# A decoder block on one core: the prologue re-ordered so that attention scores begin behind the first two chunks' layer norms

## The chip, the core and the metric

The kernel runs on one core of a Trainium2 chip. The core has five instruction streams that run side by side and wait for one another through semaphores: TensorE (PE, matrix products and transposes), VectorE (DVE), ScalarE (ACT), GpSimd (POOL), and SyncE (SP, which issues transfers). ACT issues transfers too, from the same stream as its arithmetic. The metric is the device time of one launch in microseconds (us), as a median over runs. The trace is of one profiled launch.

## The reference

`x` is 2 x 1024 x 256 in float32, so 2048 tokens. Three layers follow one another, each added to `x`:

```
n  = layernorm(x)
q, k, v = n Wq, n Wk, n Wv                      (16 heads of 16)
x += affine_layernorm( (softmax(q k^T / 16) + bias[rel]) v )
n  = layernorm(x);  k2, v2 = ctx Wk2, ctx Wv2   (ctx: 2 x 77 x 256)
x += (softmax(mask(n Wq2 k2^T)) v2) Wu + bu
n  = layernorm(x)
x += affine_layernorm( 0.5 gelu(n Ws + bs) + sum over the best 2 of 8 experts of weight * expert(n) )
```

The bias of the first layer is drawn from a table by relative position. The mask of the second layer says which of the 77 context rows count.

## The kernel before, in words

The 2048 tokens lie in SBUF in `xs` as four chunks of 512 (chunks 0 and 1 are batch 0, chunks 2 and 3 batch 1). A chunk's layer norm has these steps: `bn_stats` and `bn_aggr` on DVE give mean and variance, a power of -0.5 on POOL gives the reciprocal deviation (`norm_scale`, L133), the chunk is scaled into a tile `xn`, and `turned` (L188) turns `xn` on PE in two halves, `kc` 0 and 1, and copies each into `xnT`. There are two forms of the scaling: `scale_tokens` (L310) on DVE with the mean and the deviation, and `offsets` (L166) on DVE followed by `scale` (L177) on ACT.

Self-attention is split into 16 units (batch, group of four heads, half of the queries) of eight steps, so 128 steps. Stream A of a step (`stream_a`, L518) makes four scores `sA` on PE, and DVE takes each one's row maximum into `mx` (L533). Ten steps later (`LAG`) stream B makes the scores again, turned and shifted by the maxima (`sB`, L572), ACT takes the exponentials into tiles `pt` (L580), and `times_v` (L584) multiplies them with the values `vaug`. The queries shifted by the maxima, `qB` (L555), are made once in eight steps.

On PE, DVE, ACT and POOL the order of the program text is the order of execution: these four run under a schedule written by hand (`manual_schedule`, L239). Whatever stands ahead of the step loop is the prologue. The table `between` (L905) names the jobs that stand ahead of the scores of a step, inside the loop. All PSUM tiles come from one ring of eight banks in order of use (`one`, L83), so a bank that has not been emptied holds up the PE stream.

The prologue before: transfers are issued on SP and ACT (L245 to L261), `vaug` is cleared by DVE and POOL, constants are made from the identity matrix (`own`, `extra`, `use`, `hsel`), the weights of queries and keys are rearranged by ACT (L282), chunks 0 and 1 are normed and turned, keys and queries of the first four groups are projected (`project`, L490: `wk` and `wq`, each in column halves `j` 0 and 1). Then come the rest of the loads with the bias table (`rest_of_loads`, L288), the mask (`mask_bias`, L472), and keys and values of the context (`context_turn`, `context_keys`, `context_values`). Only then does step 0 begin. Between steps 0 and 7 stand the values of all chunks (`values`, L329) and the layer norms of chunks 2 and 3. `add_values` (L352) sums the values on POOL for the flat part of the bias.

The tiles `cx`, `cwk`, `cwv`, `wv`, `mk` and the raw weights live in a pool `fst` that is closed in step 9; the pool of `pt`, `avs` and `part` then takes the same memory, so that its first users wait for the last users and the loads of `fst`.

A load takes one of eight semaphores in turn; a load that comes eight places later waits until the earlier one has landed.

Of the kernel before, what the change touches and what calls it, by code (L numbers as in the profile page):

```python
# [11 lines left out]
ALU = mybir.AluOpType  # L12
# [3 lines left out]
B = 2  # L16
S = 1024
D = 256
H = 16
DH = 16  # L20
N = B * S
NT = N // P
QT = S // P
# [12 lines left out]
FLAT = 510  # L36
# [4 lines left out]
def decoder_kernel(  # L41
# [27 lines left out]
    nc = tc.nc  # L69
# [17 lines left out]
    moments, tokens = {}, {}  # L87
# [9 lines left out]
    def load_x(c):  # L97
        nc.sync.dma_start(
            out=xs[:, 4 * c : 4 * c + 4, :],
            in_=xf[512 * c : 512 * c + 512, :].rearrange("(t p) d -> p t d", p=P),  # L100
        )

    def load_rows(src, name, cols, pool=const, eng=nc.scalar):
        t = pool.tile([P, 2, cols], F32, name=name)
        eng.dma_start(out=t, in_=src.rearrange("(kc p) f -> p kc f", p=P))
        return t
# [6 lines left out]
    def load_heads(src, name, pool, eng):  # L113
        t = pool.tile([P, 2, H, DH], F32, name=name)
        for kc in range(2):
            eng.dma_start(  # L116
                out=t[:, kc, :, :], in_=src[:, kc * P : (kc + 1) * P, :].rearrange("h p k -> p h k")
            )
        return t.rearrange("p kc h k -> p kc (h k)")
# [42 lines left out]
    def deviation(c, eps=1e-5):  # L162

        tokens[c] = norm_scale(moments[c][1], 4, eps)
# [81 lines left out]
    for name, src in (("wk", a_wk), ("wq", a_wq)):  # L246
        raws[name] = load_rows(src, f"{name}raw", D, fst)
    load_x(1)
    cx = fst.tile([P, B, D], F32, name="cx")
    for b in range(B):  # L250
        nc.sync.dma_start(out=cx[:T2, b, :], in_=context[b])
    cwk = load_heads(c_wk, "cwk", fst, nc.scalar)
    load_x(2)
    cwv = load_heads(c_wv, "cwv", fst, nc.scalar)
    wv = load_rows(a_wv, "wv", D, fst)
    load_x(3)
    for a in range(8):
        nc.sync.dma_start(out=flat_of[16 * a : 16 * a + 16, :], in_=a_relT[:, FLAT : FLAT + 1])
    mk = fst.tile([P, NT, T2], I32, name="mk")
    nc.sync.dma_start(out=mk, in_=mask.rearrange("b (t p) k -> p (b t) k", p=P))  # L260
    beta_a = load_bcast(a_beta, "beta_a")  # L261

    nc.vector.memset(vaug[:, : QT // 2], 0.0)
    nc.gpsimd.memset(vaug[:, QT // 2 :], 0.0)
    nc.gpsimd.memset(vaug.rearrange("p k h r b -> p (k h) r b")[:, :, DH, :], 1.0)
    i32 = ident.rearrange("p (g r) -> p g r", r=32)
    for i in range(2):
        nc.vector.tensor_reduce(own[i], i32[:, :, DH * i : DH * i + DH], AX.XY, ALU.add)
# [2 lines left out]
    nc.vector.tensor_reduce(  # L271
        hsel, ident.rearrange("p (a j r) -> p j a r", a=2, j=4), AX.XY, ALU.add
    )
    nc.vector.tensor_scalar(hsel, hsel, 0.25, None, ALU.mult)
    for name, raw in raws.items():
        c0 = {"wk": 2048, "wq": 2560}[name]
        w = scrap[:, c0 : c0 + 512].rearrange(
# [10 lines left out]
    def rest_of_loads():  # L288
        nc.vector.tensor_copy(tab[:, FLAT - 7 :], flat_of.to_broadcast([P, M_TAB - FLAT + 7]))
        for a in range(8):  # L290
            nc.sync.dma_start(
                out=tab[16 * a : 16 * a + 16, : FLAT + 1 - a], in_=a_relT[:, a : FLAT + 1]
            )
        for m in shifts:
            nc.gpsimd.memset(m, 0.0)
        nc.gpsimd.memset(vx, 0.0)
# [9 lines left out]
    def measure_tokens(c):  # L306
        mv = stats(xs[:, 4 * c : 4 * c + 4, :], 4)
        tokens[c] = mv, norm_scale(mv, 4, 1e-5)

    def scale_tokens(c):  # L310
        mv, r = tokens[c]
        xn = work.tile([P, 4, D], F32, tag="xn", name="xn")
        for t in range(4):
            nc.vector.tensor_scalar(
                xn[:, t, :],
                xs[:, 4 * c + t, :],
                mv[:, t, 0:1],
                r[:, t : t + 1],
                ALU.subtract,
                ALU.mult,  # L320
            )
        tokens[c] = mv, r, xn

    def turn_tokens(c):

        for kc in range(2):
            turned(c, kc, by_dve if kc == 0 and c < 2 else by_act)

    def values(c, u):  # L329

# [139 lines left out]
            )  # L470

    def mask_bias():  # L472
        nc.vector.tensor_scalar(mb, mk, 0, -1000000000.0, ALU.is_equal, ALU.mult)
        nc.vector.tensor_reduce(live, mb, AX.X, ALU.max)
        nc.vector.tensor_scalar(live, live, 0.0, None, ALU.is_ge)

# [409 lines left out]
    def shared(c, u):  # L886
# [16 lines left out]


    between = {  # L905
        0: [lambda: values(0, 0)],
        1: [lambda: values(0, 1), lambda: measure_tokens(2)],
        2: [lambda: values(1, 0), lambda: scale_tokens(2), lambda: turn_tokens(2)],
        3: [lambda: values(1, 1), lambda: measure_tokens(3)],
        4: [lambda: values(2, 0), lambda: scale_tokens(3), lambda: turn_tokens(3)],  # L910
        5: [lambda: values(2, 1)],
        6: [lambda: values(3, 0)],
        7: [lambda: values(3, 1), add_values],
        16: [flat_bias],
        20: [lambda: bias_half(2, 0)],
        22: [lambda: bias_half(2, 1)],
# [3 lines left out]
        30: [lambda: bias_turn(3, 0), lambda: bias_turn(3, 1)],  # L920
    }
    between.update({40 + 4 * c: [lambda c=c: add_rows(c, beta_a)] for c in range(4)})
    measure_tokens(0)
    scale_tokens(0)
    turn_tokens(0)
    measure_tokens(1)
    scale_tokens(1)
    project(0, "wk", 0)
    project(0, "wq", 0)
    turn_tokens(1)  # L930
    project(0, "wk", 1)
# [643 lines left out]
```

## Time and profile before

| | |
|---|---|
| runs | 1022.87, 1023.93, 1017.91 us; median 1022.87 |
| profiled launch | 1017.8 us, its span 1016.1 us |
| granted PE clock, mean | 0.95 |
| busy: PE, DVE, ACT, POOL | 897.9, 604.8, 529.4, 398.5 us |
| prologue, up to the first values product | 31.79 us |
| first product of stream B (`sB`) | starts at 70.38 us |

The share of busy time says which engine has most work in the mean over the span; it is no answer for the first 70 us, which this change touches. There, read the timeline and the chain of waits: a line of the timeline gives start, duration, engine, line of the kernel, operation, tile written and tiles read, the count of merged instructions, and in brackets the idle time ahead and who ended it. A `q` behind an engine's name (ACTq, SPq) is its sequencer at issuing a transfer.

### The profile page before, as it was taken

What the parts mean: (1) busy time and instruction counts of PE and PEld (TensorE: products, weight loads), DVE (VectorE), ACT (ScalarE), POOL (GpSimd) and SP (SyncE); (2) the same over time, 40 slices, a digit from 0 to 9 for tenths busy, and PEclk for the clock granted to TensorE, in tenths of its full rate; (3) what the DMA queues carried; (4) which work ended last, traced back from release to release, by engine and by line L of the source; (5) the groups of instructions that cost most, each with busy time, mean ns of one, the idle gap of its engine ahead of it and who ended that gap; (6) DMA issues with size and microseconds to landing.
All of it is one profiled execution on the core that took longest, in us unless ns stands there. A gap on an engine that the chain in (4) does not pass through costs nothing.

```text
span 1016.1 us, 15875 instructions
## 1 busy us (share of the span) xinstructions
PE 897.9 (88%) x5948; PEld 520.5 (51%) x5948; DVE 604.8 (60%) x1197; ACT 529.4 (52%) x1051; POOL 398.5 (39%) x321
## 2 busy tenths in 40 slices
PE   3889999999999999999965999997999999998900
PEld 1553334333333333333323667786887888887800
DVE  6787558877888887987689998670110110101157
ACT  1327568867887787786852777413232222233301
POOL 3032223443334354344366897004334422222124
PEclk9989999999999999999985999998999999999955
DMA  8200000000000000000000000127446446699252
GB/s 175 48 1 1 2 1 2 1 2 1 2 1 2 1 1 2 1 1 2 1 1 17 2 22 22 43 78 280 148 175 213 160 168 201 224 321 325 80 170 83
DMA packets 65143, 75.62 MB, mean 74 GB/s; under 512 B 17948, under 2 KB 57017, under 8 KB 65057
## 3 DMA queue, kind: packets, MB, share of 16 engines
q1 hardware_dynamic: 50512, 62.31, 19.0%
q0 software_dynamic: 3360, 8.79, 2.3%
q10 hardware_dynamic: 11184, 3.41, 1.4%
q8 instruction: 50, 0.82, 0.3%
q14 instruction: 37, 0.30, 0.1%
HBM read 66.10 MB, written 8.78 MB: 74 GB/s over the span
## 4 chain that ended last, share of the span: by engine, by line
PE 69%; DVE 17%; DMA 8%; ACT 2%; ACTq 2%; issue 1%; POOL 1%; POOLq 0%; DVEq 0%; SPq 0%
PE sA L526 14%; PE av L589 12%; PE sB L572 11%; PE ph L1419 9%; PE po L1438 9%; DMA pairs<-y,to_row 7%; PE pp L496 3%; DVE mx L533 2%; DVE cs L689 2%; DVE cm L677 2%; DVE scrap L1513 1%; PE pb L390 1%; DVE scrap L673 1%; ACTq L116 1%; PE pq L641 1%
## 5 line engine op out<-in xcount | busy, mean ns | idle before, releaser
L533 DVE TENSOR_REDUCE mx<-sA 128x1 f32<-128x512 f32 x512 | 317.8, 683 | 75.2 <-PE sB L572 64.3
L580 ACT ACTIVATE pt<-sB 128x512 f32<-128x512 f32 x512 | 264.5, 603 | 86.3 <-PE sB L572 86.2
L526 PE MATMUL sA<-kT,scrap 32*128 32x512 f32 x1024 | 260.4, 625 | 0.0
L572 PE MATMUL sB<-qB,kT 32*128 32x512 f32 x1024 | 249.2, 621 | 0.0
L602 POOL TENSOR_TENSOR avs<-avs,part 128x512 f32<-128x512 f32 x112 | 142.3, 1270 | 272.3 <-ACT part L601 267.0
L1426 ACT ACTIVATE hT<-ph,b1s 128x256 f32<-128x256 f32 (+1 forms) x184 | 77.8, 424 | 185.2 <-PE ph L1419 179.4
L526 PEld LDWEIGHTS sA<-kT,scrap 32*128 32x128 f32 x1024 | 102.8, 185 | 86.6 <-ACT pt L580 52.3
L1438 PE MATMUL po<-w,hT 128*128 128x256 f32 x560 | 137.2, 382 | 7.4 <-DVE y L1445 5.5
L1419 PE MATMUL ph<-xgT,w 128*128 128x256 f32 (+1 forms) x736 | 139.0, 335 | 2.2 <-ACT hT L1426 2.1
L589 PE MATMUL av<-pt,vaug 128*32 128x512 f32 x1024 | 137.4, 605 | 0.8 <-DVE mx L533 0.8
L1419 PEld LDWEIGHTS ph<-xgT,w 128*128 128x128 f32 x736 | 116.8, 191 | 26.8 <-ACT hT L1426 11.2
L1445 DVE TENSOR_TENSOR y<-po,b 128x512 f32<-128x512 f32 (+1 forms) x23 | 13.0, 564 | 185.7 <-PE po L1438 178.7
L572 PEld LDWEIGHTS sB<-qB,kT 32*128 32x128 f32 x1024 | 99.0, 185 | 39.0 <-issue 30.4
L1438 PEld LDWEIGHTS po<-w,hT 128*128 128x128 f32 x560 | 100.4, 190 | 21.7 <-DVE y L1445 8.6
L1449 POOL DMA_INDIRECT pairs<-y,to_row x35 | 35.3, 1009 | 119.9 <-DMA pairs<-y,to_row 75.3
L1393 POOL DMA_INDIRECT xg<-xnd,from_row x35 | 34.3, 979 | 103.1 <-PE px L1409 63.2
L589 PEld LDWEIGHTS av<-pt,vaug 128*32 128x32 f32 x1024 | 21.0, 109 | 97.8 <-DVE mx L533 85.1
L601 ACT COPY part<-av 128x512 f32<-128x512 f32 x108 | 65.7, 608 | 7.2 <-PE av L589 7.2
L137 POOL TENSOR_TENSOR rstd<-rstd,nhalf 128x4 f32<-128x4 f32 x20 | 21.4, 1070 | 78.2 <-DVE rstd L136 78.1
L193 PE MATMUL pxT<-ident,xn 128*128 128x128 f32 x96 | 19.2, 315 | 32.1 <-ACT xn L183 16.5
L496 PE MATMUL pp<-xnT,scrap 128*128 128x512 f32 x64 | 32.8, 642 | 5.3 <-ACT scrap L282 4.9
L706 ACT COPY PT<-ppT 77x512 f32<-77x512 f32 x64 | 32.6, 587 | 3.0 <-PE ppT L705 2.3
(241 smaller groups left out, 963.1 us busy)
## 6 DMA issues: line engine op xcount, KB each, us to landing
w<-in_L_ffn_W_dram SPq DMA_DIRECT2D x46, 1024.0 KB, 9.0
b<-in_L_ffn_b_dram SPq DMA_DIRECT2D x23, 128.0 KB, 6.5
xs<-in_x_dram SPq DMA_DIRECT2D x4, 512.0 KB
xnd<-xn SPq DMA_DIRECT2D x4, 512.0 KB, 4.2
w<-pairs SPq DMA_DIRECT2D x4, 512.0 KB
w<-pairs ACTq DMA_DIRECT2D x4, 512.0 KB, 10.0
out_dram<-scrap SPq DMA_DIRECT2D x4, 512.0 KB, 2.9
mk<-in_mask_BxSxS_ik_dram SPq DMA_DIRECT2D x1, 616.0 KB, 4.8
```

Source lines behind the costliest of these rows:

```text
L496: nc.tensor.matmul(pp, lhsT=wqk[name][:, kc, P * G : P * G + P], rhs=xnT[:, kc, b * S + 512 * j : b * S + 512 * j + 512], start=(kc == 0), ...
L526: nc.tensor.matmul(s, lhsT=units[h // 4, "q"][r0 : r0 + 32, q0 : q0 + P], rhs=units[h // 4, "k", g % 2][r0 : r0 + 32, 512 * kh : 512 * kh ...
L533: nc.vector.tensor_reduce(largest[h][:, qt, hh : hh + 1, kh], s, AX.X, ALU.max)
L572: nc.tensor.matmul(s, lhsT=units[h // 4, "k", g % 2][r0 : r0 + 32, kt * P : (kt + 1) * P], rhs=shifted[h][r0 : r0 + 32, :], start=True, st ...
L580: nc.scalar.activation(powers[m, hh], s, AF.Exp, scale=1.0 / 16.0)
L589: nc.tensor.matmul(av[32 * hh : 32 * hh + 32, :], lhsT=vaug[:, kt, 4 * g + hh, :, b], rhs=powers.pop((m, hh)), start=True, stop=True,)
L601: copy(part, av)
L602: nc.gpsimd.tensor_tensor(sums[h], sums[h], part, ALU.add)
L1419: nc.tensor.matmul(ph[:, hc % group, :], lhsT=w1[:, kc, hc * P : (hc + 1) * P], rhs=xgT[:, kc, :], start=(kc == 0), stop=(kc == 1),)
L1426: hidden[i] = nc.scalar.activation(hT[:, hc, :], ph[:, hc % group, :], AF.Gelu, bias=b1s[:, i, hc : hc + 1])
L1438: nc.tensor.matmul(po[:, s, :], lhsT=hT[:, hc, s * P : (s + 1) * P], rhs=w2[:, hc, :], start=(hc == 0), stop=(hc == NH - 1),)
L1449: nc.gpsimd.indirect_dma_start(out=pairs[:, :], out_offset=bass.IndirectOffsetOnAxis(ap=to_row[:, k : k + 1], axis=0), in_=y[:, s, :], in_ ...
```

## The change

Transfers. `cx` moves from the third place on SP to behind `x` and `flat_of`. `cwk`, `cwv` and `wv` move from ACT to SP; `wv` comes third there, `cwk` and `cwv` behind `cx`. ACT keeps the two raw weights `wk` and `wq`.

Clearing `vaug`. One DVE memset and two POOL memsets of the whole tile go. In place of them `clear(kt)` clears on POOL, for two of the eight key tiles at a time, only the elements that no value fills; it stands between steps 1 to 4. The zeroes of `shifts` and `vx` move into `clear_rest`, step 5.

Layer norms. The statistics and deviations of chunks 0 and 1 now stand ahead of chunk 0's scaling. Chunk 0 is scaled by DVE as before; chunks 1 to 3 are scaled by ACT (`offsets` and `scale`). The steps of chunks 2 and 3 are spread over steps 0 to 6.

Moved out of the prologue: `project(0, "wq", 1)` to step 2, `rest_of_loads` to step 4, the context's turn, keys and values to steps 7, 8 and 9, the mask to step 8 and from DVE to POOL, `add_values` to step 10. The two operations that find rows with a live mask (`find_live`) stay on DVE, at step 34. The factor 0.25 on `hsel` moves from DVE to ACT.

```diff
     load_x(1)
+    wv = load_rows(a_wv, "wv", D, fst, nc.sync)
+    load_x(2)
+    load_x(3)
+    for a in range(8):
+        nc.sync.dma_start(out=flat_of[16 * a : 16 * a + 16, :], in_=a_relT[:, FLAT : FLAT + 1])
     cx = fst.tile([P, B, D], F32, name="cx")
     for b in range(B):
         nc.sync.dma_start(out=cx[:T2, b, :], in_=context[b])
-    cwk = load_heads(c_wk, "cwk", fst, nc.scalar)
-    load_x(2)
-    cwv = load_heads(c_wv, "cwv", fst, nc.scalar)
-    wv = load_rows(a_wv, "wv", D, fst)
-    load_x(3)
-    for a in range(8):
-        nc.sync.dma_start(out=flat_of[16 * a : 16 * a + 16, :], in_=a_relT[:, FLAT : FLAT + 1])
+    cwk = load_heads(c_wk, "cwk", fst, nc.sync)
+    cwv = load_heads(c_wv, "cwv", fst, nc.sync)
...
-    nc.vector.memset(vaug[:, : QT // 2], 0.0)
-    nc.gpsimd.memset(vaug[:, QT // 2 :], 0.0)
-    nc.gpsimd.memset(vaug.rearrange("p k h r b -> p (k h) r b")[:, :, DH, :], 1.0)
...
-    nc.vector.tensor_scalar(hsel, hsel, 0.25, None, ALU.mult)
+    nc.scalar.mul(hsel, hsel, 0.25)
...
+    def clear(kt):
+        part = vaug[:, kt : kt + 2]
+        for k in range(2):
+            nc.gpsimd.memset(part[:, k, :, DH:, :], 0.0)
+            nc.gpsimd.memset(part[:, k, :, DH, :], 1.0)
+    def clear_rest():
         for m in shifts:
             nc.gpsimd.memset(m, 0.0)
         nc.gpsimd.memset(vx, 0.0)
...
     def mask_bias():
-        nc.vector.tensor_scalar(mb, mk, 0, -1000000000.0, ALU.is_equal, ALU.mult)
+        nc.gpsimd.tensor_scalar(mb, mk, 0, -1000000000.0, ALU.is_equal, ALU.mult)
+    def find_live():
         nc.vector.tensor_reduce(live, mb, AX.X, ALU.max)
         nc.vector.tensor_scalar(live, live, 0.0, None, ALU.is_ge)
...
-        0: [lambda: values(0, 0)],
-        1: [lambda: values(0, 1), lambda: measure_tokens(2)],
-        2: [lambda: values(1, 0), lambda: scale_tokens(2), lambda: turn_tokens(2)],
-        3: [lambda: values(1, 1), lambda: measure_tokens(3)],
-        4: [lambda: values(2, 0), lambda: scale_tokens(3), lambda: turn_tokens(3)],
-        5: [lambda: values(2, 1)],
-        6: [lambda: values(3, 0)],
-        7: [lambda: values(3, 1), add_values],
+        0: [lambda: values(0, 0), lambda: measure(2)],
+        1: [lambda: values(0, 1), lambda: deviation(2), lambda: clear(0)],
+        2: [lambda: values(1, 0), lambda: project(0, "wq", 1), lambda: offsets(2), lambda: clear(2)],
+        3: [lambda: values(1, 1), lambda: scale(2), lambda: measure(3), lambda: clear(4)],
+        4: [
+            lambda: turned(2, 0, by_act), lambda: turned(2, 1, by_act), lambda: deviation(3),
+            lambda: clear(6), rest_of_loads,
+        ],
+        5: [lambda: values(2, 0), lambda: offsets(3), lambda: scale(3), clear_rest],
+        6: [lambda: values(2, 1), lambda: turned(3, 0, by_act), lambda: turned(3, 1, by_act)],
+        7: [lambda: values(3, 0), context_turn, lambda: context_keys(0)],
+        8: [lambda: values(3, 1), lambda: context_keys(1), mask_bias],
+        9: [lambda: context_values(0), lambda: context_values(1)],
+        10: [add_values],
+        34: [find_live],
...
-    measure_tokens(0)
+    measure(0)
+    deviation(0)
+    measure(1)
+    deviation(1)
     scale_tokens(0)
-    turn_tokens(0)
-    measure_tokens(1)
-    scale_tokens(1)
+    turned(0, 0, by_dve)
+    turned(0, 1, by_act)
+    offsets(1)
+    scale(1)
     project(0, "wk", 0)
     project(0, "wq", 0)
-    turn_tokens(1)
+    turned(1, 0, by_dve)
+    turned(1, 1, by_act)
     project(0, "wk", 1)
-    project(0, "wq", 1)
-    rest_of_loads()
-    mask_bias()
-    context_turn()
-    for G in range(2):
-        context_keys(G)
-    for b in range(B):
-        context_values(b)
```

More of the change, by code (lines that the diff above doesn't have):

```diff
@@ L304, in decoder_kernel @@
     nc.sync.dma_start(out=cwu, in_=c_wu.rearrange("(kc p) f -> p kc f", p=P))
-    def measure_tokens(c):
-        mv = stats(xs[:, 4 * c : 4 * c + 4, :], 4)
-        tokens[c] = mv, norm_scale(mv, 4, 1e-5)
     def scale_tokens(c):
-        mv, r = tokens[c]
+        mv, r = moments.pop(c)[1], tokens[c]
         xn = work.tile([P, 4, D], F32, tag="xn", name="xn")
@@ L322, in scale_tokens @@
         tokens[c] = mv, r, xn
-    def turn_tokens(c):
-        for kc in range(2):
-            turned(c, kc, by_dve if kc == 0 and c < 2 else by_act)
     def values(c, u):
```

## The prediction

> **What bounds the kernel now.** I read the table of stretches first, to see where PE is not the limit, then the chain of waits and the timeline of the first 75 us.
>
> The stretches (start, end and length, then busy us and count for PE, its weight loads, DVE, ACT, POOL; granted clock, DMA share, GB/s):
>
> ```profile
> 0.00:33.60 33.60, 17.32 (x60) 9.88 (x60) 20.01 (x45) 8.50 (x26) 8.53 (x14) 1.00 0.83 166
> 33.60:70.40 36.80, 29.42 (x162) 16.32 (x161) 29.90 (x65) 6.94 (x12) 10.83 (x9) 0.98 0.01 3
> 70.40:140.00 69.60, 69.60 (x549) 28.20 (x552) 47.30 (x78) 45.93 (x91) 15.91 (x13) 0.96 0.00 1
> ```
>
> From 70.4 us on PE has no gap; the next stretches to 495 us are nearly the same (98.5 to 100% busy). So an earlier start of stream B moves all that follows by the same amount, and what the change can win lies ahead of 70.4 us: PE idles 16.3 us in the prologue and 7.4 us in steps 0 to 9.
>
> The chain of waits, in order of time, names the owner of the prologue:
>
> ```profile
> 2.43 5.81 ACTq L116
> ...
> 8.27 1.53 ACTq L116
> ...
> 9.84 3.27 ACTq L116
> ...
> 13.16 2.67 ACTq L105
> ...
> 15.86 1.28 ACT L282
> ...
> 17.51 5.49 PE pp L496 x8
> ```
>
> ACT issues `cwk`, `cwv`, `wv` until 15.83, then loads its table and rearranges the weights; PE, whose transposes of chunk 0 ended at 12.57, waits 4.9 us for that.
>
> The timeline shows the stalls in the steps, and what else I price from:
>
> ```profile
> 9.16 1.14 SPq L98 DMA_DIRECT2D xs<-in_x_dram  x2
> 9.80 1.38 DVE L314 TENSOR_SCALAR xn<-xs,bnmv,rstd 128x256 f32<-128x256 f32 x4 [1.16 <-POOL rstd L137]
> 15.90 2.72 DVE L314 TENSOR_SCALAR xn<-xs,bnmv,rstd 128x256 f32<-128x256 f32 x4 [1.13 <-POOL rstd L137]
> 22.82 4.12 SPq L116 DMA_DIRECT2D cwq<-in_L_xattn_Wq_dram  x2
> 42.36 1.73 PE L193 MATMUL pxT<-ident,xn 128*128 128x128 f32 x8 [2.69 <-DVE xn L314]
> 52.76 1.73 PE L193 MATMUL pxT<-ident,xn 128*128 128x128 f32 x8 [2.68 <-DVE xn L314]
> 67.19 2.48 DVE L533 TENSOR_REDUCE mx<-sA 128x1 f32<-128x512 f32 x4
> 67.42 0.63 PE L552 MATMUL pm<-ident,shift 128*128 128x128 f32 x4 [2.01 <-DVE shift L541]
> 69.59 0.74 DVE L555 SCALAR_TENSOR_TENSOR qB<-scrap,use,pm 128x512 f32<-128x512 f32 x1
> ```
>
> Twice PE waits 2.7 us for a layer norm that stands behind score maxima on DVE, and once 2.0 us for the shift: 7.4 us, all of the idle time. Then `qB` waits for DVE's backlog, some 1.2 us more.
>
> **What the Trainium skill says.** "TensorE: Matmul & The Clock Gate", Part 1: after idling PE runs at half rate until some 3.4 us of activity. The trace agrees: the projections that begin at 17.51 take about 1.0 us a pass at first, 0.43 later. "SBUF — State Buffer", two separate sides: a DVE operation in its two-port mode and a POOL operation lock each other out. The trace agrees: the second `xn` above ran beside POOL memsets and took 2.72 against 1.38 us. "DMA: Bandwidth & Descriptors", queues, rings and completion order: SP and ACT each own a row of rings on the same 16 engines, served in turn. No run here shows the turns, but SP's wait for `wq` (3.2 us, until 9.16) fits two rows that share. "GPSIMD Engine Reference", key points: DVE is about twice as fast as POOL in elementwise work; that prices the mask below.
>
> **The change part by part.**
>
> *ACT freed.* Its issues end at 1.85 us. Table load (1.28), `hsel` and the eight copies of L282 (0.29 each) follow as the weights land: about 5.6 us for `wk` (SP's wait for it ends there), `wq` by 9.2. Both are ready before the turn of chunk 0, so the 4.9 us go. What is late next is the layer norm of chunk 0.
>
> *Chunk 0 behind chunk 1's statistics.* DVE's memset (3.5 us) goes; the constants take 1.0. Chunk 0 can be measured when it has landed: by 6.2 us, since DVE read it then without a wait; not before 5.6, as it is twice `wk`. I take 6.0. Statistics 2.25 and 0.2, the same for chunk 1, then scaling 1.38: `xn` from 10.95 (before: 9.80). If chunk 1 has not landed by 8.4, this waits; I add 0.3. POOL's small power may stand in the scaling's way; 0 to 1.3, I take 0. Turning starts at 11.7 and takes 2.3 cold; the copies give the first projection 13.9 (before: 17.51).
>
> *Projections.* PE stays busy from 11.7, so it warms near 15.2: two passes of 1.0, the rest 0.43 to 0.7: `wk` 3.0, `wq` 1.72, to 18.7. ACT scales chunk 1 meanwhile: 4 x 0.59 (this line's later instances) from 14.5, done at 17. Transposes 1.04, copy and latency 0.3 to 0.7, `wk` half 1 1.72: 21.8. Then the first values product, before at 31.79: **10.0 us earlier**. In this are the 1.72 of `wq` half 1 and 4.0 of the context (27.76 to 31.79) that now stand later.
>
> *Steps 0 to 9.* Before: 31.79 to 70.38, 38.6 us, of which PE idles 7.4 + 1.2, so 30.0 of work. After: plus `wq` 1.72, plus context 0.43 + 1.32 + 1.73 = 3.5, so 35.2. Idle: the norms of chunks 2 and 3 are now spread, but ACT's scaling (2.36) stands right ahead of the turn. In step 3 it starts behind the copy of `values(1,1)` and ends some 2 us behind the scores, so about 1.0 is left; in step 6 about 0.3; 0.6 between the context's turn and its keys. The 2.0 before the shift is filled by the context values (1.73), and DVE, with PE given 5.2 us more per ten steps, has no backlog at `qB`. I add 0.7 for ring banks: DVE has 10 x 2.48 + 2 x 2.5 + 0.4 = 30.2 of work, less than PE. Sum 37.8: **0.8 us less** than before. `sB` at 59.6, against 70.38.
>
> *POOL.* Clears: eight of 512 elements (0.52 each, the row of `shift`) and eight small ones (0.1): 5. They follow chunk 2's deviation and precede chunk 3's, which is needed near 41 us; done by 35. Zeroes 2.1, to about 44. Mask: from the page 2 x 0.79 = 1.6 (an estimate); bounds 1.3 (memset pace, 1232 elements) and 5 (POOL's adds take 2.5 ns an element, and this converts integers as well). It must end before the first exponential near 60 us, 11 us later even at the slow bound: cost nothing. `add_values` 8.9, done by 64, used in step 16.
>
> *SP.* `cwk` and `cwv` carry their slow issue with them: 4 issues of about 2.1 to 3 us (the two of `cwq` took 4.12; ACT's four 11.3). Ahead of them stand `flat_of` x8, each waiting for a load eight places back, to about 12 us. So `cwv` is issued by 24 and `mk` lands by 30 (4.8 to landing), well before steps 7 to 9 (46 us on); the tail of SP moves by 12 us and is used much later. The table's eight loads wait for DVE's copy in step 4 and land by 47; used in step 20. Cost nothing; cover 10 us and more.
>
> *`find_live` on DVE in step 34:* 1.44 + 0.17 us. DVE idles about 0.45 us a step there, the ring holds less than a step: cost 0 to 1.6, I take 0.4. Taking the mask off DVE in the prologue wins nothing, PE was the later one.
>
> Sum: 10.0 + 0.8 - 0.4 = **10.4 us** off 1017.8, so 1007.4 for a launch like the profiled one. That one is as fast as the lowest run (1017.91); against the median, 1022.87 - 10.4 = **1012.5 us**.
>
> **The rivals.** *Loads late* (0.18): SP now queues `wv`, `x2`, `x3` at once behind `x0` and `x1`: 2.75 MB with the weights. If the engines do not take them in order, chunk 1 lands at 10 to 11 us (300 to 380 GB/s in the table of stretches by two microseconds), DVE in order holds chunk 0's scaling behind it, and 2 to 4 us are lost: 1015.5. For it: `wq` landed as late as 9.16. Against: `cwk`'s small packets were among the traffic then. *The change does less than it says in the steps* (0.10): PE, DVE and ACT wait for one another at each layer norm as before, and the 5.2 us of moved PE work just come on top: 10.0 - 6 = 4 won, 1019. Against it: the maxima no longer stand between statistics and scaling. *More than forecast* (0.16): chunk 0 lands by 5.6, no bank stalls, `find_live` hidden: 13 won, 1010. For it: each of my additions (0.3, 0.7, 0.4) was a precaution. Against: the norms of chunks 2 and 3 were never seen in this place. *Slower* (0.06): the mask on POOL becomes the bound. It stands behind clears and zeroes, waits for `mk` at SP's tail, and the first `pt` takes its memory. It begins to cost when it ends after 60 us and outweighs all gains after 70 us, so if the operation takes above 26 us (21 ns an element); at 30 us the kernel takes 1026. Against it: that is eight times the slowest POOL row.
>
> **How the numbers follow.** My forecast has 0.50, the rivals the chances above. One per cent, about what a measurement can tell from no change, is 10.2 us, and my sum lies on that edge: of the forecast's 0.50, 0.28 lies beyond it, of *more* all 0.16: faster 0.44. Of *slower*, 0.05 is beyond one per cent on the other side; the rest, 0.51, lies within. The range takes in the late loads and half of the smaller gain above, and below the larger gain and the low baseline run: 1006 to 1019.
>
> **What would show it.** ACT's first copy of L282 near 6 us; the first projection near 13.9, the first values near 21.8, `sB` near 59.6; transposes in steps 4 and 6 with under 1.2 us of idle; no POOL or DMA release ahead of the first exponential; the rest unchanged in length. Wrong would make it: DVE waiting for chunk 1, a PE clock that stays low through the first steps, or a POOL mask of over 16 us.

## The result, and the profile after

The changed kernel takes 1005.52 us (median of 4 runs, 1004.62 to 1007.79) where the kernel before took 1020.39 us beside it (1015.55 to 1023.93): a ratio of 0.9864, 95% interval 0.9836 to 0.9892. It is faster by over one per cent. The forecast had been 1012.5 us in a range of 1006 to 1019 us, made against a median of 1022.87; the measured median lies half a us below that range, but the kernel before was itself 2.5 us faster here, and the ratio lies inside (1006 / 1022.87 is 0.9835). Profile against profile, where single marks can be compared, the forecast was 10.4 us off 1017.8, and the changed kernel's profiled launch took 1004.62 us (span 1002.9): 13.2 us off. Between the medians lie 14.9 us.

Stretches of the changed kernel, with the columns of the table shown of before (start, end and length, then busy us and count of PE, its weight loads, DVE, ACT and POOL; granted clock, DMA share, GB/s). The first three have the borders of before; the last two are the prologue up to the first values product, and the stretch from there to the first `sB`:

```profile
0.00:33.60 33.60, 21.99 (x83) 11.94 (x84) 18.67 (x55) 9.40 (x21) 7.46 (x22) 1.00 0.79 161
33.60:70.40 36.80, 35.48 (x199) 19.53 (x199) 29.98 (x58) 19.05 (x43) 17.43 (x17) 1.00 0.03 8
70.40:140.00 69.60, 69.60 (x611) 25.55 (x614) 41.75 (x70) 44.60 (x89) 18.43 (x15) 1.00 0.01 2
...
0.00:22.42 22.42, 10.81 (x28) 5.51 (x29) 9.75 (x34) 7.01 (x17) 3.02 (x9) 1.00 0.82 187
22.42:58.62 36.20, 34.88 (x190) 20.91 (x190) 28.95 (x61) 14.93 (x34) 21.88 (x29) 1.00 0.25 41
```

In steps 0 to 9 PE idled 7.4 us before (31.79 to 70.38 us), and 1.3 us now (22.42 to 58.62). The prologue ends at 22.42 instead of 31.79 us. Of these 9.4 us, 4.0 are the earlier start of the first projection (13.56 instead of 17.51); the other 5.4 are for the most part products that now stand in the steps. Stream B begins at 58.62 instead of 70.38.

The chain of waits of the changed kernel (start, duration, what) names the new owner of the prologue:

```profile
0.80 5.21 DMA xs<-in_x_dram
...
10.87 0.33 DVE xn L316
11.24 2.30 PE pxT L193 x8
13.56 5.82 PE pp L495 x8
19.38 0.45 PE pxT L193 x4
19.86 0.70 DVE xnT L196
20.60 1.98 PE pp L495 x4
22.58 1.73 PE pv L333 x8
...
35.53 2.08 ACT xn L183 x4
...
55.32 1.88 PE pcv L456 x8
57.20 0.44 PE pm L551 x4
```

No step of ACT's transfers or weight copies is left in it. It runs from the landing of chunk 0 through the statistics and the norm to PE, and from 11.24 us on it is nearly all PE, until ACT's scaling of chunk 2 interrupts it at 35.53. The values product of the context (`pcv`) fills the place ahead of `pm` where PE had waited for the shift.

The timeline of the changed kernel, in the lines that answer to the prediction's steps:

```profile
5.75 0.90 ACT L279 COPY scrap<-wkraw 128x128 f32<-128x128 f32 x4 [2.36 <-DMA wkraw<-in_L_attn_Wk_dram]
6.04 0.43 DVE L159 BATCH_NORM_STATS2 bnst<-xs 128x6 f32<-128x256 f32 x1 [3.57 <-DMA xs<-in_x_dram]
10.78 1.38 DVE L316 TENSOR_SCALAR xn<-xs,bnmv,rstd 128x256 f32<-128x256 f32 x4
13.56 5.82 PE L495 MATMUL pp<-xnT,scrap 128*128 128x512 f32 x8
22.42 1.89 PE L333 MATMUL pv<-wv,xnT 128*128 128x256 f32 x8
44.46 4.40 POOL L470 TENSOR_SCALAR mb<-mk 128x1232 f32<-128x1232 int32 x1
49.93 0.79 PE L439 MATMUL pk<-cxT,cwk 128*128 128x154 f32 x4 [0.73 <-ACT cxT L434]
160.89 1.43 DVE L473 TENSOR_REDUCE live<-mb 128x16 f32<-128x1232 f32 x1
```

DVE waits for chunk 0 until 6.04 and then does not wait for chunk 1, whose statistics follow without a gap. The mask takes 4.40 us on POOL and is done at 48.86, 11 us ahead of the first exponential at 60.13.

The gain by marks, before minus after: first values product 9.4 us; first `sB` 11.8; flat bias (`pflat`) 12.2 (92.4 to 80.2); fourth making of `qB` 12.2; fifth 11.3; end of the span 13.2. (The recorded expectations call these two makings the fifth and sixth; the first five in the changed kernel start at 57.75, 86.77, 124.42, 157.44 and 183.25 us.) From 70 to 75 us PE's granted clock was at half before and at full after:

```profile
70.00:75.00 5.00, 5.00 (x23) 3.81 (x25) 4.72 (x9) 2.17 (x4) 0.00 (x0) 0.50 0.01 2
```

```profile
70.00:75.00 5.00, 5.00 (x42) 1.71 (x42) 4.13 (x7) 3.85 (x8) 1.26 (x1) 1.00 0.00 0
```

### The profile page after: what moved, and what is told of

It reads as the page before. It is cut to its first block, busy times and chain, and to the rows that moved or that the text cites. A ratio compares the mean times of both kernels' runs of the same rounds, so it can differ in the third digit from the quotient of the medians.

```text
span 1002.9 us, 15898 instructions
## 1 busy us (share of the span) xinstructions
PE 894.6 (89%) x5948; PEld 516.9 (52%) x5948; DVE 594.9 (59%) x1185; ACT 536.1 (53%) x1064; POOL 403.9 (40%) x336
## 4 chain that ended last, share of the span: by engine, by line
PE 53%; DVE 14%; DMA 13%; issue 11%; POOL 6%; ACT 2%; POOLq 0%; ACTq 0%; DVEq 0%; SPq 0%
PE sA L525 15%; PE av L588 12%; DMA pairs<-y,to_row 11%; PE sB L571 11%; PE pp L495 3%; POOL pairs L1452 2%; PE pv L333 2%; DVE scrap L1516 2%; PE pb L387 1%; DVE cm L676 1%; PE ph L1422 1%; POOL xg L1396 1%; DVE cs L688 1%; PE pq L640 1%; DVE scrap L672 1%
## 5 line engine op out<-in xcount | busy, mean ns | idle before, releaser
L1422 PEld LDWEIGHTS ph<-xgT,w 128*128 128x128 f32 x736 | 117.5, 193 | 26.7 <-ACT hT L1429 11.3
L1441 PEld LDWEIGHTS po<-w,hT 128*128 128x128 f32 x560 | 101.5, 192 | 21.3 <-DVE y L1448 8.3
```

Of the source, the lines that this page charges most:

```text
L1422: nc.tensor.matmul(ph[:, hc % group, :], lhsT=w1[:, kc, hc * P : (hc + 1) * P], rhs=xgT[:, kc, :], start=(kc == 0), stop=(kc == 1),)
L1441: nc.tensor.matmul(po[:, s, :], lhsT=hT[:, hc, s * P : (s + 1) * P], rhs=w2[:, hc, :], start=(hc == 0), stop=(hc == NH - 1),)
```

## The experiments

All medians below stand beside runs of the kernel before on the same chip. The totals move by several us for a reason that comes up where the context stands in the prologue and where chunk 0 comes first, so most verdicts rest on marks in the trace: the first values product (`pv`), the first `sB`, and `pflat`, which starts step 16. Each mark is from one trace per kernel. Four traces whose kernels differ in nothing that PE waits for ahead of `sB` (the changed kernel twice, the search for live rows six steps earlier, the longer mask) have `pv` between 21.3 and 22.6 and `sB` between 57.5 and 58.8 us, so a difference below 1.3 us at one mark tells nothing.

**The transfers alone.** The kernel before, with the changed order and queues of the loads and nothing else:

```
-    cwk = load_heads(c_wk, "cwk", fst, nc.scalar)
...
-    wv = load_rows(a_wv, "wv", D, fst)
...
+    wv = load_rows(a_wv, "wv", D, fst, nc.sync)
...
+    cwk = load_heads(c_wk, "cwk", fst, nc.sync)
```

> The kernel before with only the order and the queues of its loads changed to those of the changed kernel. If ACT's issuing owned the prologue (my step): ACT's first weight copy comes as the weights land, near 6 us, the first projection near 13 us instead of 17.51; chunk 1's scaling on DVE (beside the POOL memsets) then becomes late, so stream B starts 4 to 5 us earlier, near 66 us, and the kernel takes 4 to 5 us less. If the loads were the true limit (rival: loads late): the first projection stays at 16 us or later and less than 1.5 us is won.

Measured: 1015.79 us, ratio 0.9968 (0.993 to 1.0005). ACT's copies begin at 5.8 and the first projection at 12.6 us, 4.9 earlier. But `pv` comes at 30.2 (1.6 earlier), `sB` at 70.2 and `pflat` at 92.6: nothing is won at the marks that count, where 4 to 5 us had been expected. The timeline of this kernel shows what is late next:

```profile
15.90 2.90 DVE L314 TENSOR_SCALAR xn<-xs,bnmv,rstd 128x256 f32<-128x256 f32 x4 [1.13 <-POOL rstd L137]
17.89 1.73 PE L193 MATMUL pxT<-ident,xn 128*128 128x128 f32 x8 [0.87 <-DVE xn L314]
20.89 5.40 PE L496 MATMUL pp<-xnT,scrap 128*128 128x512 f32 x8 [1.27 <-DVE xnT L196]
40.72 2.30 PE L193 MATMUL pxT<-ident,xn 128*128 128x128 f32 x8 [2.68 <-DVE xn L314]
```

Chunk 1's norm still ends where it did, because DVE does its statistics in order behind chunk 0's; the second eight projections run into a cold clock, that is, PE at half speed behind idle time (5.40 against 3.70 us before); and the turn of chunk 2 waits for DVE as before, and now turns at half speed (2.30 against 1.73). The freed ACT was the first link of a chain, and the second one held the time.

**All but the spread norms.** The changed kernel, with the norms of chunks 2 and 3 in their old form and place:

```
-        0: [lambda: values(0, 0), lambda: measure(2)],
-        1: [lambda: values(0, 1), lambda: deviation(2), lambda: clear(0)],
...
+        1: [lambda: values(0, 1), lambda: measure_tokens(2), lambda: clear(0)],
+        2: [
+            lambda: values(1, 0), lambda: project(0, "wq", 1), lambda: scale_tokens(2),
+            lambda: turn_tokens(2), lambda: clear(2),
+        ],
```

> The changed kernel with the layer norms of chunks 2 and 3 in their old form: statistics in steps 1 and 3, scaling on DVE in steps 2 and 4 right ahead of the turn. If spreading the norms is what took the two waits of 2.7 us: the turns of chunks 2 and 3 again have 2 to 2.7 us of PE idle time each and the kernel takes 3 to 5 us more than the changed one, stream B at 62 to 63 us instead of 58.6. If the freed time is lost elsewhere (rival: the change does less than it says in the steps): within 1 us of the changed kernel.

Measured: 1016.55 us, ratio 0.9983 (0.996 to 1.0005). `pv` still comes at 22.4, but `sB` at 69.0 and `pflat` at 90.5, some 10.4 us later than in the changed kernel: the prologue's whole gain is lost within ten steps, where a loss of 3 to 5 us was expected. The median lies 11.0 us above the changed kernel's as well. The stretch and the timeline of this kernel:

```profile
22.40:69.00 46.60, 39.41 (x191) 22.62 (x190) 34.46 (x67) 11.25 (x26) 22.22 (x29) 0.89 0.18 31
```

```profile
44.64 2.58 DVE L316 TENSOR_SCALAR xn<-xs,bnmv,rstd 128x256 f32<-128x256 f32 x4
45.38 0.48 PE L193 MATMUL pxT<-ident,xn 128*128 128x128 f32 x1 [4.44 <-DVE xn L316]
```

PE idles 7.2 us and, at a mean clock of 0.89, is busy 4.5 us longer with the same work (39.41 against 34.88). Chunk 3's turn waits 4.44 us for a scaling on DVE that stands behind the statistics and two sets of maxima and runs beside POOL's clears (2.58 against 1.38 us).

**The spread norms alone.** The kernel before with the norms of chunks 2 and 3 as in the changed one:

```
-        1: [lambda: values(0, 1), lambda: measure_tokens(2)],
-        2: [lambda: values(1, 0), lambda: scale_tokens(2), lambda: turn_tokens(2)],
...
+        1: [lambda: values(0, 1), lambda: deviation(2)],
+        2: [lambda: values(1, 0), lambda: offsets(2)],
+        3: [lambda: values(1, 1), lambda: scale(2), lambda: measure(3)],
```

> The kernel before, with the layer norms of chunks 2 and 3 spread over steps 0 to 6 as in the changed kernel (statistics, deviation, offsets, scaling on ACT, turn in steps of their own; the values products one step later) and nothing else of the change. Theory that the spread norms are the larger part of the gain in any surroundings: steps 0 to 9 take 33.5 to 35 instead of 38.6 us, 'sB' at 65.5 to 67, 'pflat' 3.5 to 4.5 earlier than 92.4, total 1016 us. Rival, that they only keep the prologue's gain from being lost and win nothing by themselves: 'sB' at 69.5 to 70.5, no change.

Measured: 1011.84 us, ratio 0.9877 (0.9815 to 0.9939). `pv` at 32.1, `sB` at 64.1 (6.3 earlier), `pflat` at 86.5 (5.9 earlier). The stretch from `pv` to `sB`, first of the kernel before, then of this one:

```profile
31.79:70.38 38.59, 31.21 (x168) 17.63 (x166) 29.88 (x65) 7.86 (x18) 10.83 (x9) 0.98 0.03 7
```

```profile
32.10:64.14 32.04, 30.74 (x167) 17.66 (x167) 26.12 (x55) 11.83 (x26) 10.87 (x9) 1.00 0.01 4
```

With the same products, PE's idle time falls from 7.4 to 1.3 us. The rival falls, and the size expected (3.5 to 4.5) was too small: the wait for the shift, which the prediction had left to the context's product, goes as well. The spread norms are the largest part of the change among those tried alone, and the only one shown to win more than 1.5 us by itself. The edit does two things at once, it spreads the steps and it moves the scaling from DVE to ACT; how the 6.3 us divide between these was not tested.

**POOL's clears out of the way.** The second experiment's kernel, with the clears moved into the prologue, to see how much of its loss is the lock between POOL and DVE:

```
-        3: [lambda: values(1, 1), lambda: measure_tokens(3), lambda: clear(4)],
+        3: [lambda: values(1, 1), lambda: measure_tokens(3)],
...
+    for kt in (0, 2, 4, 6):
+        clear(kt)
     project(0, "wk", 0)
```

> The changed kernel with the layer norms of chunks 2 and 3 in their old form, as in the earlier run, and POOL's clears of the values moved from steps 1 to 4 to the prologue, so that they do not run beside DVE's scaling. Theory that the lock between POOL's memsets and DVE's scaling carries part of that run's loss of 10.4 us: the scalings of chunks 2 and 3 take 1.37 each instead of 1.97 and 2.58, 'sB' at 66 to 67 instead of 69.0. Rival, DVE's order alone and the clock that falls in PE's waits: the scalings shorter, but 'sB' at 68.3 or later.

Measured: 1015.19 us, ratio 0.9922 (0.989 to 0.9953); `sB` at 69.6, `pflat` at 91.2. Neither theory fits. Chunk 2's scaling takes 1.37 us as expected, but chunk 3's takes 5.79, since POOL, free of the clears, has come to the zeroes and the mask by then. From the timeline of this kernel:

```profile
42.82 5.79 DVE L316 TENSOR_SCALAR xn<-xs,bnmv,rstd 128x256 f32<-128x256 f32 x4
43.41 4.41 POOL L478 TENSOR_SCALAR mb<-mk 128x1232 f32<-128x1232 int32 x1
48.02 1.97 PE L193 MATMUL pxT<-ident,xn 128*128 128x128 f32 x7 [3.91 <-DVE xn L316]
```

5.79 - 1.38 = 4.41 us, the length of the mask to a hundredth, and all of it in one of the scaling's four operations (4.46 us, the others about 0.4): DVE stood still until POOL was done. So the lock is real, and worth more here than in the second experiment, where the two scalings took 0.6 and 1.2 us longer beside the clears. How the rest of that experiment's loss divides between DVE's order and the clock stays open. In the changed kernel ACT scales these chunks, and POOL's clears, zeroes and mask meet no such operation: moving POOL's work into the steps depends on moving the scaling off DVE.

**The context in the prologue.** The changed kernel, with the context's turn, keys and values ahead of step 0:

```
-        7: [lambda: values(3, 0), context_turn, lambda: context_keys(0)],
-        8: [lambda: values(3, 1), lambda: context_keys(1), mask_bias],
-        9: [lambda: context_values(0), lambda: context_values(1)],
+        7: [lambda: values(3, 0)],
+        8: [lambda: values(3, 1), mask_bias],
```

> The changed kernel with the context's turn, keys and values back ahead of step 0 (the zeroes of their tile too). If that work only pays where it lies in the gap ahead of the shift: the first values product comes some 4 us later (more if cwv has not landed by 24 us), the gap ahead of the shift is back (2 us of PE idle), and since PE's clock is at half for 5 us behind such a gap in the trace of before, another 2 us are lost: 3 to 5 us more than the changed kernel. If moving it is neutral (PE does the same work either way and the clock is no matter of it): within 1 us.

Measured: 1010.08 us, ratio 0.9906 (0.9872 to 0.9939). `pv` is 2.6 us later (25.0), but `sB` comes at 58.8 and `pflat` at 80.1, within 0.2 of the changed kernel. From the timeline of this kernel:

```profile
55.50 0.42 PEld L551 LDWEIGHTS pm<-ident,shift 128*128 128x128 f32 x4 [0.76 <-DVE shift L540]
58.78 0.69 PE L571 MATMUL sB<-qB,kT 32*128 32x512 f32 x1 [0.71 <-DVE qB L554]
```

PE (`pm` by its weight load, PEld) gets through the steps sooner and then waits at their end, for the shift and for `qB`; at this point DVE's maxima set the pace. The context's move is neutral here, as far as one trace can tell: its first eight projections took 4.54 us instead of 5.82, by chance, which hides up to 1.3 us of what the move costs at `pv`. The total is 4.6 us above the changed kernel's all the same. Of the 5.7 us between the two profiles, 4.4 arise between 622 and 682 us, in code that none of the edits touches.

**The gap filled in the kernel before.** The kernel before, with the context's values moved to step 9 alone:

```
+        9: [lambda: context_values(0), lambda: context_values(1)],
...
-    for b in range(B):
-        context_values(b)
```

> The kernel before with only the context values moved from the prologue to step 9, into the 2.0 us that PE waits for the shift. Work hidden in the gap wins 1.7 us, no more. If the gap also costs the clock (in the trace of before the granted clock is 0.50 from 70 to 75 us, in the changed one 1.00), the clock stays at 1.00 there and 3.5 to 4.5 us are won, to near 1015 for a launch of 1018 before.

Measured: 1017.62 us, ratio 0.9974 (0.9955 to 0.9993). `sB` at 69.8, `pflat` at 91.0 (1.4 earlier), the clock at 1.00 from 70 to 75 us. The 1.7 us of product are hidden and little else comes of it, so the theory of a costly half clock falls: the half clock there had cost 0.4 to 0.8 us (from `sB` to `pflat` it takes 22.0 us before, 21.6 in the changed kernel and 21.2 here).

**The changed kernel again.**

> The changed kernel once more, on the chip of the three runs beside it, as their base. Both theories: the median between 1003 and 1009 us; first values product at 22.4, the first product with the shift ('sB') at 58.6, flat bias at 80.2, the fifth 'qB' at 157.4 and the sixth at 183.3 us, each within 0.3. If the 2 us that the changed kernel gains between 570 and 690 us are the PE clock's and not the change's, they vary from run to run: 'px' (677.2 in the first profile) may then lie 2 to 4 us later here, with the earlier marks unmoved.

Measured: 1004.31 us (1003.35 to 1007.31), ratio 0.9848 (0.9782 to 0.9914). `pv` 22.6, `sB` 58.8, `pflat` 80.3, the first transposes of the experts' tokens (`px`) at 677.4 against 677.2. The late part came out alike in the two profiles of this kernel; that it is scatter all the same is shown by the next run but one.

**The search for live rows six steps earlier.**

```
-        34: [find_live],
...
-        28: [lambda: bias_half(3, 1)],
+        28: [lambda: bias_half(3, 1), find_live],
```

> The search for live rows stands in step 28 instead of step 34. Theory that it costs DVE's delay in step 34 (0.9 us of the way from 157.4 to 183.3): the fifth 'qB' at 157.4 and the sixth at 182.4 us, so 0.9 us less at the end, unless step 28 has no more room than step 34 and then takes 0.9 itself (fifth 'qB' at 158.3, sixth at 183.3). Rival, that the 0.9 is of another source, such as the phase in which PE and DVE meet: the sixth at 183.3 and the fifth at 157.4, no change. Total within 1 us of the changed kernel.

Measured: 1006.08 us (1004.35 to 1014.35), ratio 0.9874 (0.9794 to 0.9955). From the fourth `qB` to the fifth it takes 24.91 us, as in the kernel before (24.90), where the changed kernel takes 25.81; from the third to the fourth it takes 33.44 against 33.02. So the two operations cost 0.9 us in step 34 and 0.4 in step 28: 0.5 is won, which the total can't tell. In this run `pv` came at 21.3 us, 1.1 ahead of the changed kernel's profile, though nothing ahead of step 28 was edited: the first eight projections took 4.82 instead of 5.82 us.

**Chunk 0 first.** The changed kernel, with chunk 0's scaling ahead of chunk 1's statistics:

```
     deviation(0)
+    scale_tokens(0)
     measure(1)
     deviation(1)
-    scale_tokens(0)
```

> Chunk 0 is scaled ahead of the statistics of chunk 1. Its normed rows then start near 8.4 instead of 10.78 and its transposes near 8.9 us. Theory of the prologue as a chain (statistics of both chunks, scaling, turn, projection): the first projection starts when ACT's weights are there as well, 9.5 to 11.5 instead of 13.56, chunk 1's norm ends at the same time as before, so the second projections are held by it: first values product at 21.4 to 22.4, between 0 and 1 us won, and the same at 'sB'. Rival, PE with the cold clock is what fills the prologue: all 2.4 us are won at the first values product (20.0) and at 'sB' (56.2).

Measured: 1011.27 us (1008.4 to 1014.32), ratio 0.9897 (0.9828 to 0.9966). `xn` starts at 9.70 (it waits 1.22 us for POOL's power), the transposes at 10.16, but the first projection at 14.16, later than the 13.56 of the changed kernel: now the copy of the turned rows stands behind chunk 1's statistics on DVE. `pv` at 22.8, `sB` at 59.0, 0.2 later than in the repeated run. Neither theory had this. The other order wins nothing: what it gains at the scaling it loses at the copy.

The total is 7 us above the repeated run. Up to 622 us the two profiles run within 0.4 us of each other, then come the same products in the timeline, first of the changed kernel, then of this one:

```profile
625.90 3.64 PE L715 MATMUL pco<-PT,vx 77*32 77x512 f32 x32
631.27 3.70 PE L729 MATMUL pu<-cwu,oT 128*128 128x256 f32 x16
```

```profile
626.75 7.05 PE L715 MATMUL pco<-PT,vx 77*32 77x512 f32 x32
637.17 6.38 PE L729 MATMUL pu<-cwu,oT 128*128 128x256 f32 x16
```

From 620 to 640 us the granted clock was 1.00 in the one and 0.64 in the other. Over the kernels of this study the way from `pflat` to `px` took 597.0 to 607.2 us (before 598.1, changed 597.0), though only `find_live` was ever edited in it. This is what moves the totals.

The fall begins at one place. PE waits 1.26 us for ACT there, makes the small products with the experts' gate (`pg`), then transposes (`ppT`). First the kernel before, then the changed one:

```profile
633.87 2.24 PE L756 MATMUL pg<-fgw,xnT 128*128 128x8 f32 x16 [1.26 <-ACT xnT L196]
635.97 3.32 PE L705 MATMUL ppT<-ident,st 128*77 128x128 f32 x16
```

```profile
622.21 1.95 PE L755 MATMUL pg<-fgw,xnT 128*128 128x8 f32 x16 [1.26 <-ACT xnT L196]
624.01 1.95 PE L704 MATMUL ppT<-ident,st 128*77 128x128 f32 x16
```

In 12 of the 14 traces these `ppT` took 2.52 to 3.68 us, and in the worst the slow stretch went on for over 15 us. Only the two traces of the changed kernel got through at full speed; all eight kernels made from it, whose code is the same here, did not. So 1.7 us of the difference between the two profiles arise here, and nothing in the runs ties them to the change. Why the clock falls in one run and not in the other stays open.

**A warm PE.** The changed kernel with 28 transposes of the identity, which nobody reads, on PE ahead of chunk 0's turn:

```
+    for _ in range(4):
+        pw = one("warm")
+        for t in range(7):
+            nc.tensor.transpose(pw[:, (t % 4) * P : (t % 4) * P + P], ident, ident)
     measure(0)
```

> 28 transposes of the identity, whose results nobody reads, stand on PE ahead of chunk 0's turn, so that PE is at full clock when its transposes come. Theory that the cold clock owns the slow first projections (5.82 us for 8 passes, where 8 passes took 3.4 to 4 warm): transposes 1.0 to 1.3 us shorter, first projections 2 us shorter; first values product at 19.5 to 20.5 unless chunk 1's norm then holds the second half (its transposes began at 19.22 behind the projections; xn of chunk 1 is ready near 17), so at least at 21.3; 'sB' the same amount earlier, 57.5 to 56.5. Rival, the first projections are paced by the copies of the turned rows and weights: no change at any mark.

Measured: 1003.18 us (999.67 to 1004.11), ratio 0.9818 (0.9751 to 0.9885). `pv` at 21.6, `sB` at 57.8; but the turn took 2.30 us as ever, and the eight projections 5.11, inside what runs without the transposes show (4.54 to 5.88). The transposes ended at 6.97 and PE then idled for 4.17 us, and from 11.2 to 16 us the clock reads 0.50. The edit had not done what it was to do, so it settles nothing.

**A PE kept warm.** So the same with 56 transposes (14 to a bank), and the search for live rows in step 28:

> 56 transposes of the identity ahead of chunk 0's turn instead of the 28 that left PE idle for 4.2 us again, so that PE works until about 10.6 us (28 in 5.54 us, the rest at 0.13 each), half a microsecond before chunk 0's turn; the search for live rows in step 28. Theory of the cold clock: the turn takes 1.3 to 1.8 instead of 2.30 us, the first eight projections 3.4 to 4.0 instead of 4.8 to 5.9, and then chunk 1's scaling on ACT is next: first values product at 19.3 to 20.3 (changed kernel: 22.4 and 22.6), 'sB' at 55.6 to 56.6. Rival, the idle time is no cause and the passes wait for weights: first values product at 21.3 or later. In either case 0.5 less from the fifth 'qB' on for the search for live rows. Total 1000 to 1004 us.

Measured: 999.36 us (998.81 to 1003.42), ratio 0.9768 (0.9703 to 0.9833). Stretches from 11.2 to 16 us, of the kernel with 28 and then with 56 transposes, and the timeline of the latter:

```profile
11.20:16.00 4.80, 4.78 (x11) 2.59 (x12) 1.62 (x5) 2.52 (x5) 0.90 (x1) 0.50 0.53 72
```

```profile
11.20:16.00 4.80, 4.28 (x14) 2.19 (x15) 2.31 (x7) 2.56 (x5) 1.03 (x1) 1.00 0.55 75
```

```profile
1.43 7.69 PE L931 MATMUL warm<-ident 128*128 128x128 f32 x56 [1.43 <-POOL ident masks.py:199]
11.28 1.74 PE L193 MATMUL pxT<-ident,xn 128*128 128x128 f32 x8 [2.16 <-DVE xn L316]
13.46 3.67 PE L495 MATMUL pp<-xnT,scrap 128*128 128x512 f32 x8 [0.44 <-DVE off L172]
18.35 1.98 PE L495 MATMUL pp<-xnT,scrap 128*128 128x512 f32 x4 [0.35 <-DVE xnT L196]
```

Here the clock stayed at full over 2.16 us of idle time; this run warmed PE for longer as well as closer to the turn, so it doesn't say which of the two counts. The turn takes 1.74 us, where it took 2.30 in every other trace, and the eight projections take 3.67 us. `pv` comes at 20.2 instead of 22.4, `sB` at 56.4 instead of 58.6, `pflat` at 77.9 and the fifth `qB` at 180.5, 2.8 us ahead of the changed kernel (0.5 of it from the search for live rows). Against the four like traces named above, 1.1 to 2.4 us are won at `pv` and `sB`. The theory of the cold clock holds in its marks (`sB` had been put at 55.6 to 56.6). The first projection doesn't begin sooner: DVE's and ACT's copies of the turned rows pace that. This kernel has the lowest median of the study.

**A longer mask.** The changed kernel with the mask's operation six times in a row on POOL, 26.64 us in all:

```
-        nc.gpsimd.tensor_scalar(mb, mk, 0, -1000000000.0, ALU.is_equal, ALU.mult)
+        for _ in range(6):
+            nc.gpsimd.tensor_scalar(mb, mk, 0, -1000000000.0, ALU.is_equal, ALU.mult)
```

> The mask's operation on POOL (4.40 us) stands six times in a row instead of once: it ends near 70.9 instead of 48.85 us, which is the length (26 us) that the prediction named as the point where a slow mask would outweigh all gains. Theory that the cover ends at the first exponential (60.13) and what is later delays the stream one to one: the first exponential at 70.9, PE waits behind full score banks, 'pflat' at 89 to 91 instead of 80.2, and the total 1013 to 1017 us, near the kernel before. Rival, that PE has other work to do meanwhile or that DVE's and ACT's slack takes part of it back: 'pflat' below 86, total below 1010.

Measured: 1017.54 us (1014.26 to 1021.5), ratio 0.9953 (0.9931 to 0.9974). From the timeline of this kernel:

```profile
70.83 2.06 ACT L580 ACTIVATE pt<-sB 128x512 f32<-128x512 f32 x4 [13.47 <-POOL mb L471]
71.48 1.22 PE L572 MATMUL sB<-qB,kT 32*128 32x512 f32 x1 [8.80 <-ACT pt L580]
```

The first exponential waits for POOL until 70.83 instead of 60.13 us, PE for ACT behind full banks, and `pflat` comes at 91.0 us, 10.8 late. The cover ends where the prediction had put it, at the first exponential, and past it the delay reaches the stream one to one; at 26.6 us of mask nearly all of the change's gain at `pflat` is gone. The exponentials of this layer don't read `mb`; by the code, `pt` takes the memory of `mk`, which the mask is the last to read.

## Why the prediction was right, and where its sizes were off

*What bounds the kernel, and where to look:* right. What was won ahead of stream B stayed won: the distance between the two kernels is 12.2 us at `pflat` and 11.3 from the fifth `qB` to 560 us.

*ACT freed:* its step was right (copies at 5.75, put near 6), and "what is late next is the layer norm of chunk 0" as well. It says nothing on what the freed ACT is worth alone: nothing, at `sB` and `pflat`.

*Chunk 0 behind chunk 1's statistics:* put at 6.0, 10.95, 11.7 and 13.9 us for statistics, scaling, turn and projection; measured 6.04, 10.78, 11.24 and 13.56. The precaution of 0.3 for a late chunk 1 was not needed. The experiment that scaled chunk 0 first shows that the order, about which the prediction had not asked, loses nothing.

*Projections:* the term that was too small. The first eight products of 128 x 512 (passes) were put at 3.0 + 1.72 = 4.7 us and took 5.82; two passes were taken as cold, and about five were (0.85 us each). Of these 1.1 us the earlier start gave back 0.3; the first values product came 0.6 later than the 21.8 forecast. PE was to be warm 3.5 us behind the start of the turn, near 15.2 us; the last slow weight load (0.34 us, 0.19 later on) began at 17.11. What the cold passes cost is shown by the warm PE, which took 3.67 us. Part of it is chance: the same code took 4.54 us in one run and 5.88 in another. The Trainium skill's "TensorE: Matmul & The Clock Gate", Part 1, says that the window is free-running and the number of cold products varies from run to run, which fits. It also puts the idle time after which the clock falls at some 3.4 us. 2.16 us of idle time harmless and 4.17 us not would fit that, but other traces here don't, and they decide: half speed came behind 2.01 us in the kernel before (at 70 us), where 2.69 us had left the clock at full (at 42 us), behind 2.68 us with the transfers alone, and behind 1.26 us in the late part of 12 traces.

*Steps 0 to 9:* the term that was mis-sized most. Put at 37.8 us, measured 36.20, so 2.4 us less than before where 0.8 was forecast. By its parts: work 35.2 forecast, 34.9 measured; idle time 1.0 + 0.3 + 0.6 forecast, 1.32 measured; for the 0.7 of ring banks no idle time is left. `sB` was put at 59.6 and came at 58.62. The mechanism, norms spread out of DVE's way, was right, and the experiment with the spread norms alone shows it to be worth 6.3 us at `sB`; the prediction's sum had 6.0 of lost time going (8.6 less 2.6; of the 8.6 the trace shows 7.4 as idle time, in the other 1.2 PE was slow and counts as busy). What it gave to the context's values, the filling of the gap ahead of the shift, is not theirs: that gap goes with the norms, and where the context stands made no difference that the runs can tell.

*POOL:* the clears were to be done by 35 us, ahead of chunk 3's deviation; the last pair stands behind it in step 4 and ended at 42.7, which cost nothing. The mask was put at 1.6 us, from the factor of two that the page named there states, with an upper bound of 5. It took 4.40 us against DVE's 0.79, 5.6 times. The bound held and the cover was larger, so that the cost was nothing, as forecast. The condition on it was not seen: "SBUF — State Buffer", two separate sides, which the prediction quoted for the kernel before, would also have charged the clears and the mask to DVE's scaling, had that stayed on DVE. One run shows 4.4 us for it.

*SP:* right in that chunk 0 and ACT's two weights were the only loads waited for ahead of stream B, but its sums were too high. The four context loads were put at 2.1 to 3 us each and took 1.87 + 2.41 = 4.28 us together, against 11.2 on ACT before. The tail of SP was to move back by 12 us; `mk` was issued at 17.53, 2 us sooner than before.

*`find_live`:* 0.4 taken, 0.9 measured, inside the bounds of 0 and 1.6.

*The sum:* 10.4 forecast. Measured 9.4 in the prologue, 2.4 in the steps, 0.4 from `sB` to `pflat`, where the clock no longer falls at 70 us, less 0.9 for `find_live`: 11.3. The last 1.9 us of the 13.2 come behind 560 us. The prediction had no term for that: 1.7 of them are the clock's fall behind the idle time of 1.26 us, which the profile of the kernel before has and that of the changed kernel lacks, by luck as far as the runs show. What separates the medians beyond the profiles (14.9 against 13.2) no trace places. The chances were too low on the side of the result: a gain beyond one per cent had 0.44, a smaller one 0.51.

*The rivals:* loads that come late (chunk 1 was there by 8.44), a change that does less in the steps (it did more), and a slow mask (with 4.40 us far from its point of 26, which the longer mask confirmed) are out. The half clock of before at 70 us, which could have been a rival, was worth less than 1 us. *More than forecast* was put at 13 us off, which the profiles show almost to the number, but not for its reasons: chunk 0 was measured from 6.04 and not from 5.6, and `find_live` cost 0.9; only the bank stalls stayed away, and 1.9 us come from the late part. That number was luck.

## What to carry to other kernels

Where engines wait for one another in turn, price a change by the chain and not by the wait that it removes: freeing ACT alone won nothing to speak of, all but the spread norms won 1.4 us at the first `sB`, the spread norms alone 6.3, and all together 11.8. When a small vector job holds up the bottleneck engine, look at what stands ahead of it in its own engine's order; splitting its steps over several stages, and giving the scaling to a third engine, removed the wait without removing any work. Before POOL is given work "in the shade", check which DVE operations it will run beside, and where its result's memory is first needed.

## What had not been expected of the hardware

A comparison with multiply from int32 to float32 on 128 x 1232 elements took 4.40 us on POOL (3.6 ns an element of a partition) and 0.79 on DVE, while a POOL memset of 512 took 0.52. A DVE scaling of 1.38 us took 5.79 beside that mask. Behind 56 warm-up transposes and 2.16 us of idle time PE ran at full clock, behind 28 and 4.17 us at half; but behind 1.26 us and small products its clock fell in 12 of 14 traces. The weight loads show the cold clock as well, with 230 ns at first and 141 later for the turn. In the cold first 16 us of the changed kernel the column of the granted clock reads 1.00 all the same, while passes take 0.85 instead of 0.43 us: there the durations have to be read, not the column.
